# Layer 1's attention logits formed on TensorE in a four-layer graph network on one Trainium2 core

## The chip, the cores and the metric

The kernel runs on one core of one Trainium2 chip, as one launch. Its time is the device time of that core in microseconds; the figure of a kernel is the median over several executions. The profile is of one execution, with its own time. Its abbreviations: PE is TensorE's matmuls and PEld its weight loads, DVE is VectorE, ACT is ScalarE, POOL is GpSimd, SP is SyncE, which issues most DMAs.

## The reference

Sixteen graphs of 1024 nodes with 64 features each go through four layers, each of the form x + layer(relu(layernorm(x))). The change is in layer 1, a graph attention layer:

```
def layer1(inp, adj, W, a):                       # inp: relu(layernorm(x)), [16, 1024, 64]
    h = einsum('bnf,fo->bno', inp, W)
    lh = leaky_relu(h, negative_slope=0.2)
    f_src = lh @ a[:64, 0]
    f_dst = lh @ a[64:, 0]
    e = f_src[:, :, None] + f_dst[:, None, :]
    dj = 0.8 * adj + 0.2 * e
    attention = softmax(where(dj > 0, dj, -1e12), axis=1)
    return relu(einsum('bij,bjo->bio', attention, h))
```

So every node has two logits, f_src and f_dst, and a column j of the attention matrix is a masked softmax over the source nodes i. Layer 0 is a plain product with adj, layer 2 a hyperbolic attention layer, and layer 3 takes weighted quantiles of every node's neighbours (which the kernel does by sorting) followed by a small MLP.

## The kernel before

**Tiling.** A graph's 1024 nodes lie as 8 tiles (NT) of 128 partitions (P), features along the free dimension (C = 64). The adjacency matrix comes from memory transposed, one tile of 128 x 1024 at a time, through `Feed`, which keeps three tiles in flight. Partition p of tile J is node j = 128 J + p, and its row holds all sources i.

**Streams.** The program is written as generators, called streams, that run at build time: `heads` (layers 0, 1 and 2 of every graph, as `fast0`, `fast1` and `fast2`), `places` (drops neighbours and ranks the rest, mostly f16 matmuls into PSUM tiles pv and pd), `weigh`, `fetches` (GpSimd's indirect DMAs that gather neighbours' rows, la and hg), `hubs` and `lows` (sorting networks of `max` and `min` on VectorE, tiles ha, hb, la and lb) and `finish` (the MLP). After each piece a stream yields the tiles that it needs next. The loop at lines 2355 to 2365 always steps the ready stream with the smallest due time. A `Plan` (lines 80 to 173) books every instruction at a cost from formulas and says when a tile will be ready. A head counts as HEADS_US = 127 us of VectorE, a graph's hubs as 82, its lows as 93. Hubs and lows start 1.3 graphs behind. On each engine the instructions then stand in exactly the order in which they were laid out (`Queue`), and the real waits are semaphores.

**Gates.** Layer 2 of a graph waits until its ranking is done (`T.ranked > b`, line 1655), which `places` does beside layer 1; fetches of a graph wait until its head is done (`T.headed > b`); lows and hubs wait for what was fetched.

**Layer 1, `fast1` (line 1315).** After the layer norm, h is transposed to hT (64 x 1024), one half at a time through one PSUM tile pt. Eight matmuls with the weights wgs give ph = h W with nodes on partitions, which ScalarE copies to hp. VectorE then forms lh = max(0.2 hp, hp) and two dot products over the features (a product with a row of `a` broadcast to all partitions, asr or adr, and a reduction): fs and fd, one column per tile. fs is scaled by 0.25, and two more tiny operations give thr = -0.25 fd and fd2 = 0.2 fd. In the trace fd2 is written fd, since trailing digits are left out of names. TensorE transposes fs, broadcast along the free dimension, which puts the row of all fs on all 128 partitions; ScalarE copies it to fsr, which has hT's memory.

Then comes a loop over the tiles J of adj, software-pipelined: `attend` (one pass of VectorE, d = adj + fsr with the row's maximum mx; CUSTOM_DVE_ANT_0 in the trace, with an accumulator read behind it), `bound` (nm = min(-0.8 mx, fd2)), `exponential` (ScalarE, exp(0.8 d + nm)), `chosen` (VectorE's second pass, keeping ex where d > thr and summing it to sm), `share` (1 / sm to rs), ScalarE's hs = hp rs, and two matmuls with hs as weights into pa. In a step the first pass of column J comes before the second pass of column J - 1, and `bound` of J comes behind it:

Of the kernel before, what the change touches and what calls it, by code (L numbers as in the profile page):

```python
# [17 lines left out]
F32 = mybir.dt.float32  # L18
# [275 lines left out]
def tile_gnn_stack(  # L294
# [109 lines left out]
    def bcast_row(src, name):  # L404
        t = cp.tile([P, src.shape[-1]], F32, name=name)
        nc.sync.dma_start(t, src.partition_broadcast(P))
        return t
# [3 lines left out]
    wgs = cp.tile([C, C], F32, name="wgs")  # L411
# [7 lines left out]
    nc.sync.dma_start(w2s, w2)  # L419
    b1s = cp.tile([H, 1], F32, name="b1s")  # L420
    nc.sync.dma_start(b1s, b1)
    b0r = bcast_row(b0, "b0r")
    b2r = bcast_row(b2, "b2r")
    asr = bcast_row(ag[0], "asr")
    adr = bcast_row(ag[1], "adr")
# [5 lines left out]
    def row3(r):  # L431
        return r[:, None, :].to_broadcast([P, NT, C])
# [53 lines left out]
    def transpose_steps(dst, src, ps, tag, bufs):  # L486

        R, pts = src.shape[2], []
        for hf in range(2):
            pt = ps.tile([P, HN], F32, tag=tag, name="pt")  # L490
            for k in range(4):
                nc.tensor.transpose(pt[:R, k * P:(k + 1) * P], src[:, 4 * hf + k, :], ident)
            pts.append(pt)
            if hf or bufs == 1:
                for k in range(len(pts)):
                    yield [pts[k]]
                    h0 = hf if bufs == 1 else k
                    nc.scalar.copy(dst[:, h0 * HN:(h0 + 1) * HN], pts[k][:R, :])
                pts = []
# [773 lines left out]
    def halves(po, lhs, rhs, J):  # L1273

        for hf in range(2):
            nc.tensor.matmul(po[64 * hf:64 * hf + 64, :], lhs, rhs[:, hf * HN:(hf + 1) * HN],
                             start=(J == 0), stop=(J == NT - 1))
# [36 lines left out]

    def fast1(feed, xt, xn):
        with tc.tile_pool(name="f1", bufs=1) as sp, tc.tile_pool(name="f1w", bufs=2) as wp, \
                tc.tile_pool(name="f1p", bufs=1, space=PSUM) as ps:
            h = sp.tile([P, NT, C], F32, name="h")
            yield from norm_steps(h, xt, sp, "ln_xc")
            hT = sp.tile([C, N], F32, tag="hT", name="hT")  # L1320
            yield from transpose_steps(hT, h, ps, "pt", 1)
            yield [hT]
            ph = ps.tile([P, NT, C], F32, name="ph")
            for t in range(NT):
                nc.tensor.matmul(ph[:, t, :], hT[:, t * P:(t + 1) * P], wgs, start=True, stop=True)
            yield [ph]
            hp = sp.tile([P, NT, C], F32, name="hp")
            nc.scalar.copy(hp, ph)
            yield [hp]
            lh = sp.tile([P, NT, C], F32, name="lh")  # L1330
            nc.vector.scalar_tensor_tensor(lh, hp, 0.2, hp, ALU.mult, ALU.max)
            fs = sp.tile([P, NT], F32, name="fs")
            dot(fs, lh, row3(asr), sp, "dot")
            fd = sp.tile([P, NT], F32, name="fd")
            dot(fd, lh, row3(adr), sp, "dot")

            nc.vector.tensor_scalar_mul(fs, fs, 0.25)
            thr = sp.tile([P, NT], F32, name="thr")
            nc.vector.tensor_scalar_mul(thr, fd, -0.25)
            fd2 = sp.tile([P, NT], F32, name="fd2")  # L1340
            nc.vector.tensor_scalar_mul(fd2, fd, 1.0 - 0.8)
            fsr = sp.tile([P, N], F32, tag="hT", name="fsr")
            for hf in range(2):
                yield [fs, fsr] if hf else [fs]
                pt = ps.tile([P, HN], F32, tag="pt", name="pt")
                for k in range(4):
                    t = 4 * hf + k
                    nc.tensor.transpose(pt[:, k * P:(k + 1) * P], fs[:, t:t + 1].to_broadcast([P, P]), ident)
                yield [pt]
                nc.scalar.copy(fsr[:, hf * HN:(hf + 1) * HN], pt)  # L1350
            yield

            pa = ps.tile([P, HN], F32, name="pa")
            mx = sp.tile([P, NT], F32, name="mx")
            nm = sp.tile([P, NT], F32, name="nm")
            sm = sp.tile([P, NT], F32, name="sm")
            def attend(J, a):
                one_ = slice(J, J + 1)
                d = wp.tile([P, N], F32, name="d")
                nc.vector.tensor_tensor_reduce(d, a, fsr, 1.0, -3.0e38, ALU.add, ALU.max, mx[:, one_])  # L1360
                return d

            def bound(J):
                one_ = slice(J, J + 1)
                nc.vector.tensor_scalar(nm[:, one_], mx[:, one_], -0.8, fd2[:, one_], ALU.mult, ALU.min)

            def exponential(J, d):
                one_ = slice(J, J + 1)
                ex = wp.tile([P, N], F32, name="ex")
                nc.scalar.activation(ex, d, AF.Exp, bias=nm[:, one_], scale=0.8)  # L1370
                return ex

            def chosen(J, d, ex):
                one_ = slice(J, J + 1)
                nc.vector.scalar_tensor_tensor(ex, d, thr[:, one_], ex, ALU.is_gt, ALU.mult, accum_out=sm[:, one_])

            def share(J):
                one_ = slice(J, J + 1)
                rs = wp.tile([P, 1], F32, name="rs")
                nc.vector.tensor_scalar_max(rs, sm[:, one_], 0.5)  # L1380
                nc.vector.reciprocal(rs, rs)
                return rs

            d = ex = None
            for J in range(NT + 1):
                e = d
                if J < NT:
                    a = feed.next()
                    yield [a, fsr] + [ex] * (J > 0)
                    d = attend(J, a)  # L1390
                elif J:
                    yield [ex]
                if J:
                    chosen(J - 1, e, ex)
                x = ex
                if J < NT:
                    bound(J)
                if J:
                    rs = share(J - 1)
                    yield [rs]  # L1400
                    hs = wp.tile([P, C], F32, name="hs")
                    nc.scalar.activation(hs, hp[:, J - 1, :], AF.Copy, scale=rs)
                if J < NT:
                    ex = exponential(J, d)
                if J:
                    yield [hs]
                    halves(pa, hs, x, J - 1)
            yield []
            z = sp.tile([P, NT], F32, name="z")
            nc.vector.tensor_scalar(z, sm, 0.5, 1.0 / N, ALU.is_lt, ALU.mult)  # L1410
            yield [z]
            pu = ps.tile([P, 1], F32, name="pu")
            for hf in range(2):
                for J in range(NT):
                    nc.tensor.matmul(pu[64 * hf:64 * hf + 64, :], hp[:, J, :], z[:, J:J + 1], start=(J == 0), stop=(J == NT - 1))
            yield [pu]
            us = sp.tile([P, 1], F32, name="us")
            nc.scalar.copy(us, pu)
            r = sp.tile([P, HN], F32, name="r")
            nc.scalar.activation(r, pa, AF.Relu, bias=us)  # L1420
            yield [r]
            po = ps.tile([P, 4, 2, C], F32, tag="ph", name="po")
            for k in range(4):
                nc.tensor.transpose(po[:, k].rearrange("p h c -> p (h c)"), r[:, k * P:(k + 1) * P], ident)
            yield
            v = "p (h k) c -> p k h c"
            nc.vector.tensor_tensor(xn.rearrange(v, h=2), po, xt.rearrange(v, h=2), ALU.add)
# [989 lines left out]
```

## Time and profile before

| | us |
|---|---|
| median of 3 runs | 5802.13 |
| lowest, highest | 5785.95, 5806.57 |
| span of the profiled execution | 5801.1 |
| granted TensorE clock, mean | 0.624 |

The groups of instructions that the change touches, with their counts over the 16 graphs (busy us in all, mean ns of one):

| group | count | busy us | mean ns |
|---|---|---|---|
| VectorE lh<-hp | 16 | 11.1 | 696 |
| VectorE dot_pr<-lh,asr and dot_pr<-lh,adr | 16 each | 11.1 each | 693, 691 |
| VectorE fs<-dot_pr and fd<-dot_pr | 16 each | 11.0 each | 686 |
| VectorE nm<-mx,fd | 128 | 26.5 | 207 |
| VectorE d<-adj,fsr (first pass) | 128 | 155.6 | 1216 |
| VectorE ex<-d,thr,ex (second pass) | 128 | 164.7 | 1287 |
| TensorE pt<-ident,fs | 128 | 32.3 | 402 |
| TensorE ph<-wgs,hT | 256 | 58.8 | 421 |

How to read it: a group is named out<-in by tiles, and a TensorE f32 matmul of the program shows as two instructions. Busy time is the sum of durations; neighbouring instructions of an engine may overlap a little, so that the distance from one start to the next can be shorter than the duration. A view in order of time lists each instruction's start and duration in us, and in brackets the idle time of its engine before it. A view of waits lists who waited for which tile of which engine: us in total, times, longest.

### The profile page before, as it was taken

Reading aid. Unit: us, or ns where it says so; the run is one execution under the profiler, and the core shown is the slowest. Engines: PE = TensorE matmul, PEld = TensorE weight load, DVE = VectorE, ACT = ScalarE, POOL = GpSimd, SP = SyncE. Lnnn points to the kernel's source line nnn. Section 1 sums busy time; section 2 is a strip of 40 time slices with the busy share of each in tenths; the row PEclk is TensorE's granted clock in tenths of the full one; section 3 lists DMA queues with packets and bytes.
Section 4 is the critical chain, followed back from the end, with each engine's and each line's share of the span. In section 5 each row is a group of like instructions: output and inputs, shape, how many; then the busy total and the mean of one; then the engine's idle time right before and its main releaser. Section 6 shows DMA issues by size and latency. Waiting matters only on the chain. (4 is left out here: it accounts for less than half of the span.)

```text
span 5801.1 us, 60310 instructions
## 1 busy us (share of the span) xinstructions
PE 3195.6 (55%) x13232; PEld 1786.9 (31%) x13233; DVE 5107.1 (88%) x13854; ACT 3240.9 (56%) x9555; POOL 3698.0 (64%) x2903
## 2 busy tenths in 40 slices
PE   6566564646746464764646656474665646566110
PEld 2334242323423233342323324233342323324000
DVE  3579989999899999899899998999989899898857
ACT  4555565656556565565556556565655556565312
POOL 0174675758657574875758667576876758677676
PEclk7766656666665666666566665666666566666555
DMA  2232322223232222322323242322323222242120
GB/s 70 63 89 62 103 59 78 70 76 89 68 88 71 75 70 63 102 68 76 77 74 72 66 103 58 78 71 71 92 68 84 67 76 69 65 104 66 30 46 15
DMA packets 460779, 419.38 MB, mean 72 GB/s; under 512 B 218067, under 2 KB 351667, under 8 KB 460404
## 3 DMA queue, kind: packets, MB, share of 16 engines
q1 hardware_dynamic: 353908, 295.94, 17.8%
q0 software_dynamic: 106496, 119.49, 10.5%
q8 instruction: 107, 1.75, 0.1%
q14 instruction: 268, 2.20, 0.1%
HBM read 363.99 MB, written 50.54 MB: 71 GB/s over the span
## 5 line engine op out<-in xcount | busy, mean ns | idle before, releaser
L187 POOL DMA_INDIRECT la<-s_hd,ix x1856 | 2405.5, 1296 | 1351.4 <-DVE ix L187 698.6
L187 POOL DMA_INDIRECT hg<-s_hd,ix x768 | 990.7, 1290 | 234.0 <-issue 211.5
L187 DVE TENSOR_TENSOR lb<-la 128x128 f32<-128x128 f32 (+14 forms) x1760 | 677.0, 438 | 83.5 <-DMA la<-s_hd,ix 44.8
L187 DVE TENSOR_TENSOR la<-lb 128x256 f32<-128x256 f32 (+11 forms) x1856 | 695.9, 431 | 51.8 <-ACT lb L187 48.1
L187 DVE TENSOR_TENSOR hb<-ha 128x128 f32<-128x128 f32 (+36 forms) x1632 | 637.4, 447 | 53.0 <-ACT ha L187 29.1
L187 DVE TENSOR_TENSOR ha<-hb 128x64 f32<-128x64 f32 (+36 forms) x1568 | 606.5, 441 | 5.0 <-ACT hb L187 4.0
L187 PE MATMUL pw<-ident,u_z 128*128 128x128 f32 x1024 | 237.4, 376 | 441.1 <-DVE u_z L187 430.0
L187 POOL DMA_INDIRECT s_vp<-vr,s_place x128 | 154.3, 1206 | 432.6 <-DVE c_sb L187 144.3
L187 PE MATMUL pm<-w,hn 128*65 128x128 f32 x2048 | 405.9, 380 | 6.1 <-DVE w L187 5.8
L187 PE MATMUL pd<-tab_r,tab_dist 67*128 67x512 f32 x512 | 381.6, 838 | 23.6 <-DVE u_g L187 12.4
L187 PEld LDWEIGHTS pm<-w,hn 128*65 128x65 f32 x2048 | 388.3, 210 | 9.4 <-DVE w L187 9.4
L187 PEld LDWEIGHTS pw<-ident,u_z 128*128 128x128 f32 x1024 | 170.5, 193 | 648.6 <-issue 573.9
L187 PE MATMUL pl<-tab_ll,tab_rl 66*128 66x512 f32 x512 | 367.4, 809 | 0.0
L187 ACT COPY hb<-ha 128x32 f32<-128x32 f32 (+24 forms) x1280 | 274.4, 284 | 144.5 <-DVE ha L187 140.6
L187 PE MATMUL pf<-vcol,one 128*1 128x3 f32 x32 | 3.1, 166 | 633.5 <-DVE vcol L187 633.5
L187 ACT ACTIVATE u_g<-pd,gxc 128x512 f32<-128x512 f32 x256 | 174.5, 682 | 315.4 <-PE pd L187 294.3
L187 ACT COPY ha<-hb 128x4 f32<-128x4 f32 (+22 forms) x1264 | 253.3, 268 | 172.6 <-DVE hb L187 169.5
L187 PE MATMUL pv<-wtile,krow 8*128 8x512 f16 x512 | 290.3, 567 | 103.4 <-ACT d L187 55.8
L187 PE MATMUL pa<-adj,h 128*64 128x512 f32 x512 | 196.8, 895 | 246.6 <-DMA adj<-in_adjt 124.3
L187 ACT COPY lb<-la 128x64 f32<-128x64 f32 (+6 forms) x784 | 195.4, 296 | 205.0 <-DVE la L187 102.8
L187 PE MATMUL pv<-wt,ng 128*128 128x128 f16 x2048 | 297.2, 295 | 0.0
L187 DVE FIND_INDEX8 ix<-seek,row 128x8 uint32<-128x1056 f16 x224 | 279.7, 1250 | 0.0
(342 smaller groups left out, 8282.0 us busy)
## 6 DMA issues: line engine op xcount, KB each, us to landing
adj<-in_adjt SPq DMA_DIRECT2D x384, 512.0 KB
la<-s_hd,ix POOLq DMA_INDIRECT x1856
row<-s_vp SPq DMA_DIRECT2D x112, 256.0 KB
hg<-s_hd,ix POOLq DMA_INDIRECT x768
wb<-wd SPq DMA_DIRECT2D x32, 342.0 KB
row<-s_vp SPq DMA_DIRECT2D x192, 28.0 KB
row<-s_vp SPq DMA_DIRECT2D x192, 24.0 KB
xa<-in_x SPq DMA_DIRECT2D x16, 256.0 KB
```

Source lines behind the costliest of these rows:

```text
L187: r = f(*a, **k)
```

## The change

The logits come from TensorE. Since leaky_relu(v) = 0.2 v + 0.8 relu(v), a logit is 0.2 (W a) . h + 0.8 a . relu(h W). One constant tile `aside` (128 x 2) holds both sets of coefficients, one above the other, already multiplied by 0.25 for the source logit and by 0.2 for the destination logit. It is made once, before the streams start, from two small loads of `a`, a transpose of W and one matmul.

In `fast1` the tile `cat` (128 x 1024) takes hT in its upper half of partitions and relu(h W), transposed, in its lower half: two matmuls with wgs as weights give (h W) transposed for 512 nodes each, and ScalarE's relu copies them. Two matmuls with a column of `aside`, broadcast as 128 equal columns, give the source logits already on all partitions, and ScalarE copies them to fsr. Eight matmuls with tiles of `cat` as weights and the other column of `aside` give the destination logits, one column each; a copy makes them fd. lh, both dot products, the three scalings and the eight transposes of fs go.

In the loop the first pass forms d = -0.8 (adj + fsr) and takes the minimum, beginning with the node's fd. Its accumulator is then nm itself, and `bound` goes. The exponential is exp(nm - d), and the second pass keeps ex where d < fd. The pool of PSUM tiles has two slots for pt, which pa uses too, where there were one for pt and one for pa.

```diff
+    aside = cp.tile([P, 2], F32, name="aside")
+    agt = ag.rearrange("k c -> c k")
+    nc.sync.dma_start(aside[C:2 * C], agt)
+    with tc.tile_pool(name="wa", bufs=1) as kp, tc.tile_pool(name="wap", bufs=1, space=PSUM) as kps:
+        a0 = kp.tile([C, 2], F32, name="a0")
+        nc.sync.dma_start(a0, agt)
+        pw = kps.tile([C, C], F32, name="pw")
+        nc.tensor.transpose(pw, wgs, ident[0:C, 0:C])
+        wgt = kp.tile([C, C], F32, name="wgt")
+        nc.scalar.copy(wgt, pw)
+        pwa = kps.tile([C, 2], F32, name="pwa")
+        nc.tensor.matmul(pwa, wgt, a0, start=True, stop=True)
+        for k, f in enumerate((0.25, 1.0 - 0.8)):
+            nc.vector.tensor_scalar_mul(aside[0:C, k:k + 1], pwa[:, k:k + 1], 0.2 * f)
+            nc.vector.tensor_scalar_mul(aside[C:2 * C, k:k + 1], aside[C:2 * C, k:k + 1], (1.0 - 0.2) * f)
...
-            hT = sp.tile([C, N], F32, tag="hT", name="hT")
-            yield from transpose_steps(hT, h, ps, "pt", 1)
-            yield [hT]
-            ph = ps.tile([P, NT, C], F32, name="ph")
+            cat = sp.tile([P, N], F32, name="cat")
+            yield from transpose_steps(cat[0:C], h, ps, "pt", 2)
+            yield [cat]
+            ph = ps.tile([P, NT, C], F32, name="ph", bufs=1)
             for t in range(NT):
-                nc.tensor.matmul(ph[:, t, :], hT[:, t * P:(t + 1) * P], wgs, start=True, stop=True)
-            yield [ph]
+                nc.tensor.matmul(ph[:, t, :], cat[0:C, t * P:(t + 1) * P], wgs, start=True, stop=True)
+            pts = []
+            for hf in range(2):
+                pt = ps.tile([P, HN], F32, tag="pt", name="pt", bufs=2)
+                nc.tensor.matmul(pt[C:2 * C, :], wgs, cat[0:C, hf * HN:(hf + 1) * HN], start=True, stop=True)
+                pts.append(pt)
+            for hf in range(2):
+                yield [pts[hf]]
+                nc.scalar.activation(cat[C:2 * C, hf * HN:(hf + 1) * HN], pts[hf][C:2 * C, :], AF.Relu)
+            yield [cat]
+            fsr = sp.tile([P, N], F32, name="fsr")
+            pts = []
+            for hf in range(2):
+                pt = ps.tile([P, HN], F32, tag="pt", name="pt", bufs=2)
+                nc.tensor.matmul(pt, aside[:, 0:1].to_broadcast([P, P]), cat[:, hf * HN:(hf + 1) * HN], start=True, stop=True)
+                pts.append(pt)
+            pf = ps.tile([P, NT], F32, tag="pu", name="pf", bufs=1)
+            for t in range(NT):
+                nc.tensor.matmul(pf[:, t:t + 1], cat[:, t * P:(t + 1) * P], aside[:, 1:2], start=True, stop=True)
+            for hf in range(2):
+                yield [pts[hf]]
+                nc.scalar.copy(fsr[:, hf * HN:(hf + 1) * HN], pts[hf])
+            yield [pf]
+            fd = sp.tile([P, NT], F32, name="fd")
+            nc.scalar.copy(fd, pf)
             hp = sp.tile([P, NT, C], F32, name="hp")
             nc.scalar.copy(hp, ph)
-            yield [hp]
-            lh = sp.tile([P, NT, C], F32, name="lh")
-            nc.vector.scalar_tensor_tensor(lh, hp, 0.2, hp, ALU.mult, ALU.max)
-            fs = sp.tile([P, NT], F32, name="fs")
-            dot(fs, lh, row3(asr), sp, "dot")
-            fd = sp.tile([P, NT], F32, name="fd")
-            dot(fd, lh, row3(adr), sp, "dot")
-
-            nc.vector.tensor_scalar_mul(fs, fs, 0.25)
-            thr = sp.tile([P, NT], F32, name="thr")
-            nc.vector.tensor_scalar_mul(thr, fd, -0.25)
-            fd2 = sp.tile([P, NT], F32, name="fd2")
-            nc.vector.tensor_scalar_mul(fd2, fd, 1.0 - 0.8)
...
-                for k in range(4):
-                    t = 4 * hf + k
-                    nc.tensor.transpose(pt[:, k * P:(k + 1) * P], fs[:, t:t + 1].to_broadcast([P, P]), ident)
-                yield [pt]
-                nc.scalar.copy(fsr[:, hf * HN:(hf + 1) * HN], pt)
-            yield
+            yield [fsr, fd]
...
-                nc.vector.tensor_tensor_reduce(d, a, fsr, 1.0, -3.0e38, ALU.add, ALU.max, mx[:, one_])
+                nc.vector.tensor_tensor_reduce(d, a, fsr, -0.8, fd[:, one_], ALU.add, ALU.min, nm[:, one_])
                 return d
-
-            def bound(J):
-                one_ = slice(J, J + 1)
-                nc.vector.tensor_scalar(nm[:, one_], mx[:, one_], -0.8, fd2[:, one_], ALU.mult, ALU.min)
...
-                nc.scalar.activation(ex, d, AF.Exp, bias=nm[:, one_], scale=0.8)
+                nc.scalar.activation(ex, d, AF.Exp, bias=nm[:, one_], scale=-1.0)
...
-                nc.vector.scalar_tensor_tensor(ex, d, thr[:, one_], ex, ALU.is_gt, ALU.mult, accum_out=sm[:, one_])
+                nc.vector.scalar_tensor_tensor(ex, d, fd[:, one_], ex, ALU.is_lt, ALU.mult, accum_out=sm[:, one_])
...
-                if J < NT:
-                    bound(J)
```

More of the change, by code (lines that the diff above doesn't have):

```diff
@@ L1316, in fast1 @@
         with tc.tile_pool(name="f1", bufs=1) as sp, tc.tile_pool(name="f1w", bufs=2) as wp, \
-                tc.tile_pool(name="f1p", bufs=1, space=PSUM) as ps:
+                tc.tile_pool(name="f1p", bufs=2, space=PSUM) as ps:
             h = sp.tile([P, NT, C], F32, name="h")
             yield from norm_steps(h, xt, sp, "ln_xc")
-            hT = sp.tile([C, N], F32, tag="hT", name="hT")
-            yield from transpose_steps(hT, h, ps, "pt", 1)
-            yield [hT]
-            ph = ps.tile([P, NT, C], F32, name="ph")
+            cat = sp.tile([P, N], F32, name="cat")
@@ L1340, in fast1 @@
-            fd2 = sp.tile([P, NT], F32, name="fd2")
-            nc.vector.tensor_scalar_mul(fd2, fd, 1.0 - 0.8)
[L1342 to L1345, printed above, removed]
-                for k in range(4):
-                    t = 4 * hf + k
-                    nc.tensor.transpose(pt[:, k * P:(k + 1) * P], fs[:, t:t + 1].to_broadcast([P, P]), ident)
-                yield [pt]
-                nc.scalar.copy(fsr[:, hf * HN:(hf + 1) * HN], pt)
@@ L1351, in fast1 @@
-            yield
-            pa = ps.tile([P, HN], F32, name="pa")
-            mx = sp.tile([P, NT], F32, name="mx")
+            yield [fsr, fd]
+            pa = ps.tile([P, HN], F32, tag="pt", name="pa", bufs=2)
             nm = sp.tile([P, NT], F32, name="nm")
@@ L1411, in fast1 @@
             yield [z]
-            pu = ps.tile([P, 1], F32, name="pu")
+            pu = ps.tile([P, 1], F32, name="pu", bufs=1)
             for hf in range(2):
@@ L1421, in fast1 @@
             yield [r]
-            po = ps.tile([P, 4, 2, C], F32, tag="ph", name="po")
+            po = ps.tile([P, 4, 2, C], F32, tag="ph", name="po", bufs=1)
             for k in range(4):
```

## The prediction

> **What bounds the kernel now.** I read the page from the top: busy shares, then the slices, then stretches of the span, then the order of time inside one graph.
>
> ```profile
> PE 3195.6 (55%) x13232; PEld 1786.9 (31%) x13233; DVE 5107.1 (88%) x13854; ACT 3240.9 (56%) x9555; POOL 3698.0 (64%) x2903
> DVE  3579989999899999899899998999989899898857
> 2000.00:2500.00 500.00, 304.14 (x1332) 164.74 (x1332) 462.94 (x1289) 302.75 (x905) 347.42 (x277) 0.62 0.30 75
> 5400.00:5801.00 401.00, 29.41 (x84) 16.39 (x84) 293.65 (x843) 110.05 (x489) 275.58 (x180) 0.50 0.16 32
> POOL la L187 <- DVE ix L187: 698.6, 26, 65.5
> 2360.00:2390.00 30.00, 25.51 (x122) 0.52 0.32 66
> ```
>
> Lines 1 and 2: VectorE is the fullest engine, and its empty slices are the first three and the last few. Line 3, a stretch of the middle (columns: PE, PEld, DVE, ACT, POOL busy, granted clock, DMA share, GB/s): 463 of 500 us on VectorE. The view of waits between 1000 and 5000 us names some 239 us of 4000 in which VectorE waited for another engine or a DMA; the rest of its gaps are fractions of a microsecond between dependent instructions. So the middle runs at VectorE's pace. The op that begins layer 1's logits (lh) starts at 1016.0 us in graph 3 and 5156.3 us in graph 15: 345 us a graph. What leaves VectorE there leaves the span. Line 4, the tail after the last head: VectorE is idle 107 us of 401, and GpSimd's row fetches pace it. Line 5: GpSimd waits 699 us in all for indices, 26 times, mostly because the next graph's head has not ended. Line 6, TensorE alone in 30 us around graph 7's logits: 25.5 busy at a granted clock of 0.52. In that stretch TensorE is nearly full. The chain of waits covers only the last 24 us (the MLP of graph 15), which the change doesn't touch.
>
> **What leaves VectorE.** Graph 7, in order of time (start, duration):
>
> ```profile
> 2374.36 0.69 DVE L187 SCALAR_TENSOR_TENSOR lh<-hp 128x512 f32<-128x512 f32 x1
> 2375.09 0.69 DVE L187 TENSOR_TENSOR dot_pr<-lh,asr 128x512 f32<-128x512 f32 x1
> 2375.81 0.69 DVE L187 TENSOR_REDUCE fs<-dot_pr 128x8 f32<-128x512 f32 x1
> 2376.53 0.69 DVE L187 TENSOR_TENSOR dot_pr<-lh,adr 128x512 f32<-128x512 f32 x1
> 2377.26 0.69 DVE L187 TENSOR_REDUCE fd<-dot_pr 128x8 f32<-128x512 f32 x1
> 2377.86 0.17 DVE L187 TENSOR_SCALAR fs<-fs 128x8 f32<-128x8 f32 x1
> 2377.98 0.17 DVE L187 TENSOR_SCALAR thr<-fd 128x8 f32<-128x8 f32 x1
> 2378.06 0.16 DVE L187 TENSOR_SCALAR fd<-fd 128x8 f32<-128x8 f32 x1
> 2378.14 0.08 DVE L187 MATCH_VALUE_LOAD ix<-seek,row 128x8 f16 x1
> ...
> 2395.05 1.27 DVE L187 SCALAR_TENSOR_TENSOR ex<-d,thr,ex 128x1024 f32<-128x1024 f32 x1
> 2396.25 0.08 DVE L187 DVE_READ_ACCUMULATOR ex<-d,thr,ex 128x1 f32 x1
> 2396.25 0.20 DVE L187 TENSOR_SCALAR nm<-mx,fd 128x1 f32<-128x1 f32 x1
> 2396.38 0.14 DVE L187 TENSOR_SCALAR rs<-sm 128x1 f32<-128x1 f32 x1
> ```
>
> All eight ops from lh to the last fd go. I count them from start to start, because neighbours overlap: 2378.14 - 2374.36 = **3.8 us a graph**. Nothing of another stream stands between them, so nothing fills the hole but the next work.
>
> [...] In columns 1 to 7 nm starts with the accumulator read and rs follows 0.13 us later; rs reads that accumulator, and where a result of the accumulator read is wanted at once (graph 7's column 0: read at 2387.32, nm at 2387.44) the reader starts 0.12 us after it. So nm sits in a gap that rs would leave anyway: about 0.01 us. Only column 0, with no such rs, frees 0.2 us. I take **0.2 us a graph**.
>
> **What VectorE gets.** Each of the 128 first passes (mean 1216 ns, CUSTOM_DVE_ANT_0) now starts its accumulation at a column of fd instead of a literal, with a minimum instead of a maximum. The trace has neither form. Lower bound 0: as many elements and passes. Upper bound by rows: rs<-sm, 128x1 with literals, 144 ns; nm, 128x1 with a column among its operands, 207 ns; so +63 ns. The second pass, which has a column operand, takes 1.20 us to its accumulator read, the first 1.15: +50 ns. I take 50 ns, 8 x 0.05 = **0.4 us a graph**; the exponential's and the second pass's other signs cost nothing.
>
> Sum on VectorE: 3.8 + 0.2 - 0.4 = 3.6 us a graph, x 16 = **58 us**. By busy durations it would be 3.95 + 1.66 - 0.4 = 5.2, x 16 = 83 us: the upper end. The lower end, with the pointer at 63 ns and the bounds at nothing, is 53 us.
>
> **What TensorE gets.** New per graph: two calls of hT by W (512 columns), two of the broadcast logit column (512 columns), eight that give the destination logit (one column each). Gone: eight transposes of fs. A 512-column f32 call of layer 2 (pd, pl) goes from start to start in 0.86 us at best and 1.58 us for the first of a row of them; at this stretch's clock of 0.52 I take 1.6, four calls 6.4 us. The eight one-column calls have a close row:
>
> ```profile
> 155.39 3.57 PE L187 MATMUL pq<-attc,tab_r 64*128 64x2 f32 x16
> ```
>
> Eight calls, each with its own 128-wide weights, two instructions per call: 3.57 us. [...] The row decides: 3.5. The transposes took 4 in 1.06 us, so 2.0 come back. Net 6.4 + 3.5 - 2.0 = **+7.9 us a graph** (4.9 at the best spacing), 126 us in all on an engine 55% busy.
>
> What waits there: TensorE's broadcast call waits for ScalarE's relu of both halves; behind it on TensorE stand the ranking matmuls (pv) of the same graph's places, behind these ScalarE's d and VectorE's rem. ScalarE's copy of fd waits for all eight one-column calls, and the first pass waits for that copy. In graph 7 the first column started 16.1 us after the first ph matmul (2370.04 to 2386.17). The new chain: ph 3.6, hT by W 3.2, last relu 0.58 (row hT<-pt), broadcasts 3.2, one-column calls 3.5, copies of fd and hp 0.7: 14.8 us, plus ranking matmuls laid between (up to 5 us). VectorE has other streams' work meanwhile, as it has now; if that cover were gone, the delay would cost up to 4 us a graph. In graphs 0 and 1, where VectorE is half idle, the two chains are equal within that, so the 3.6 us may be lost there: 7 us at most.
>
> **What else.** ScalarE: two relus of 0.58 and one small copy (0.16, row us<-pu), 1.3 us a graph on an engine 56% busy: hidden. Set-up, once: two small loads on SP (0.4 to 0.8 us of issue, before an xa load that SP issues only at 20.02, when VectorE's set-up ends), a transpose, a copy and a matmul beside POOL's set-up, four tiny VectorE ops of 0.19: +0.8 us. The logit tiles take the two slots that pt and pa had, so nothing new waits for PSUM.
>
> **The order.** The streams are laid out by booked costs, so every later instruction may move. By the code's own formulas the head is booked 3.9 us less and, if the column counts as a third operand, 1.4 more for the first passes: -2.5 of HEADS_US = 127, which stays. Heads then gain 2% on hubs and lows, up to 0.3 graph by the end. That moves 0.3 x (82 + 93) = 52 us of sorting behind the last head. If the 107 idle us of the tail take it, the gain is up to 52 us; if GpSimd's fetches, 0.3 of some 270 us a graph, are late with it, the loss is 81 - 52 = 29 us. Gates hold streams together, so I take 0.
>
> Sum against the profiled execution: 5801.1 - 58 + 0.8 = 5744; half of the first two graphs' 7 us given back, 5748. The median before, 5802.13, is 1 us above that span, so the same sum serves both.
>
> **The rivals.** (1) **Given back by the new order.** For it: GpSimd's and the tail's 29 us above, static waits of ScalarE copies (la, lb, ha: some 67 us in the middle) that may fall elsewhere. Against: VectorE's waits are 6% only. 5748 + 29 = 5777, up to 5830 if waits grow by another 53 us. (2) **TensorE's ranking stretch sets the pace.** Place: line 6 above, 85% full; places must end before layer 2 of the same graph, and GpSimd already waits for heads. Price: heads later by 7.9 us a graph, less the 3.6 that VectorE frees: 16 x 4.3 = +69, so 5870. It decides from the point where VectorE finds no sorting to do, that is where its share in the middle falls below some 91% while GpSimd's waits for indices grow. Against: that share is 92 to 93% now and sorting has buffers of up to three fetched blocks. (3) **All busy time counts**, and the tail takes the heads' lead: 5801 - 83 = 5718, down to 5690. (4) The minimum form of the pass costs a second sweep or the like, 128 x 1.2 = +154: 5900; nothing in the trace speaks for it, and it is counted within the slower chance.
>
> **How the numbers follow.** About 0.5% (29 us) can be told from no change. Forecast 5748, own range 5725 to 5772: 0.50. Rival 3: 0.12. Rival 1: 0.20, mostly within 29 us of before. Rivals 2 and 4: 0.18. Faster 0.62, same 0.20, slower 0.18. The range leaves out most of rivals 2 and 4 and the end of rival 3: 5700 to 5840.
>
> **What would show it.** VectorE busy down by about 83 us by the page though the span falls less; the custom pass at 1.21 to 1.28 us; rs still 0.12 us behind its accumulator read; one-column matmuls at 3.5 us for eight; ph-to-first-pass within 15 to 20 us; a period of some 341 us. Wrong if the pass exceeds 1.35 us, if GpSimd's waits for indices grow by over 60 us, or if the middle's VectorE share drops below 91%.

## The result and the profile after

The changed kernel takes 5834.34 us (median of 6 runs, 5819.18 to 5847.72) against 5802.58 us for the kernel before in the same job (6 runs, 5785.77 to 5808.61): ratio 1.0067, 95% interval 1.0051 to 1.0084. It is slower by 0.7%, where faster by 0.9% was forecast. The profiled execution has a span of 5845.9 us at a mean granted clock of 0.626, so 44.8 us more than before; it is the slowest of its six runs, and the medians lie 31.8 us apart.

The page of the kernel after, busy time of the engines and VectorE's slices:

```profile
PE 3287.0 (56%) x13491; PEld 1839.6 (31%) x13492; DVE 5047.6 (86%) x13602; ACT 3265.9 (56%) x9604; POOL 3624.8 (62%) x2903
DVE  3579989899898989989898898989989898998957
```

VectorE's busy time fell by 5107.1 - 5047.6 = 59.5 us. Its idle time (span less busy) rose from 694.0 to 798.3, by 104 us. The work did leave. More than that came back as gaps, and the slices show where: in the middle every second or third digit is now an 8.

The stretches (columns: length, PE, PEld, DVE, ACT, POOL busy, granted clock, DMA share, GB/s). Line 1 is the middle of the kernel before. The others are of the kernel after: the middle, one stretch of it, the tail, 30 us around graph 7's logits, and the densest stretch of graph 7's ranking:

```profile
1000.00:5000.00 4000.00, 2354.91 (x9676) 1313.75 (x9675) 3672.86 (x9917) 2346.25 (x6843) 2680.78 (x2101) 0.62 0.30 76
1000.00:5000.00 4000.00, 2381.22 (x9815) 1334.30 (x9814) 3600.15 (x9698) 2345.70 (x6868) 2599.05 (x2095) 0.63 0.29 75
2000.00:2500.00 500.00, 308.83 (x1297) 163.50 (x1297) 450.55 (x1229) 283.93 (x857) 342.37 (x271) 0.63 0.31 83
5400.00:5845.90 445.90, 68.37 (x239) 43.80 (x237) 332.26 (x923) 130.78 (x535) 296.40 (x207) 0.53 0.16 34
2410.00:2440.00 30.00, 24.59 (x100) 13.06 (x100) 25.93 (x67) 21.69 (x47) 24.52 (x19) 0.57 0.28 67
2476.00:2513.00 37.00, 35.98 (x160) 18.93 (x160) 33.46 (x79) 18.01 (x41) 28.77 (x28) 0.50 0.21 47
```

VectorE's share of the middle is 90.0%; before it was 3672.9 of 4000 us, 91.8%. The tail starts later (the last head ends 61 us later) but is itself 16 us shorter. In line 5, around graph 7's logits as in the prediction, TensorE is no fuller than before (24.59 us against 25.51). Line 6 is a stretch that the prediction did not consider: 35.98 of 37 us busy at a granted clock of 0.50.

VectorE's waits between 1000 and 5000 us, with GpSimd's wait for indices over the whole run from the same view (us in all, times, longest):

```profile
DVE la L187 <- ACT lb L187: 74.7, 54, 2.4
DVE lb L187 <- DMA la<-s_hd,ix: 40.2, 13, 4.4
DVE v_a L187 <- ACT v_l L187: 38.5, 12, 4.7
...
DVE rt_r L187 <- ACT rt_s L187: 31.2, 24, 2.4
...
POOL la L187 <- DVE ix L187: 810.2, 18, 59.1
```

Before, these four of VectorE were 22, 0, 6 and 5 us, and GpSimd's wait was 698.6. All of VectorE's named waits in the middle add to 309 us, against 239 before. No single wait holds the loss. VectorE waits more for ScalarE's copies and for fetched rows, and GpSimd waits 112 us more for the next head: the heads come later.

So I measured the heads stage by stage: distances between the first instructions of each stage, mean over graphs 3 to 14, in us. Layer 1 runs from its layer norm to its last operation. The ranking goes on beside it: its first part runs from its first to its second group of pc matmuls, its second part from there to the last copy to krow. The MLP counts as inside when its last matmuls (py) begin there.

| | before | after |
|---|---|---|
| period | 345.3 | 348.3 |
| layer 1 | 109.3 | 113.3 |
| layer 2 waits, after layer 1's last operation | 2.6 | 9.9 |
| layer 2 | 187.5 | 180.5 |
| from there to the next layer 1 | 45.9 | 44.7 |
| ranking, first part | 65.6 | 74.7 |
| ranking, second part | 40.7 | 50.5 |
| graphs (of 16) with the MLP inside the second part | 1 | 14 |

The four rows below the period add up to it. It grows by 3.0 us, 48 us over 16 graphs, near the 44.8 us between the profiled executions. Layer 1 is 4.0 us longer, layer 2's wait for the ranking 7.3 us longer, and layer 2 itself 7.0 us shorter. The last row points to a cause of the wait. The MLP is that of an earlier, finished graph (`finish`), and the change doesn't touch it. Here is TensorE in order of time in graph 7 of the kernel after (start, duration):

```profile
2476.99 1.92 PE L187 MATMUL pt<-ident,ga 128*64 128x128 f32 x8 [2.00 <-DVE ga L187]
2478.83 2.07 PE L187 MATMUL ph<-ot,w1s 64*128 64x512 f32 x2
2480.84 0.60 PE L187 MATMUL pv<-wtile,krow 8*128 8x512 f16 x1
...
2482.98 2.07 PE L187 MATMUL ph<-ot,w1s 64*128 64x512 f32 x2
...
2489.03 3.68 PE L187 MATMUL py<-w2s,hid 128*128 128x64 f32 x16
2492.64 0.60 PE L187 MATMUL pv<-wtile,krow 8*128 8x512 f16 x1
...
2516.67 1.94 PE L187 MATMUL pk<-ident,n_key 128*128 128x128 f32 x8 [3.71 <-DVE n_key L187]
```

The rows with ga, w1s and w2s are the MLP: 1.92 + 2.07 + 2.07 + 3.68 = 9.74 us, between ranking matmuls (pv) that stand back to back from 2478.8 to 2513. The ranking's second part is 50.5 - 40.7 = 9.8 us longer. Its beginning does have gaps: over the whole second part, in the mean of graphs 3 to 14, TensorE is busy 83% at a granted clock of 0.61 (82% at 0.63 before). In the kernel before, the last matmuls of graph 7's ranking and its MLP's py were these:

```profile
2459.95 1.94 PE L187 MATMUL pk<-ident,n_key 128*128 128x128 f32 x8 [1.30 <-DVE n_key L187]
L187 PE MATMUL py<-w2s,hid x16: 315/421/421, 2490.2 to 2493.3; 128*128 128x64 f32 x16
```

The ranking's matmuls ended at 2461.9, and py began 28 us later, beside layer 2, where no one waited for it.

### The profile page after: what moved, and what is told of

It reads as the page before. It is cut to its first block, busy times and chain, and to the rows that moved or that the text cites. A ratio compares the mean times of both kernels' runs of the same rounds, so it can differ in the third digit from the quotient of the medians.

```text
span 5845.9 us, 60160 instructions
## 1 busy us (share of the span) xinstructions
PE 3287.0 (56%) x13491; PEld 1839.6 (31%) x13492; DVE 5047.6 (86%) x13602; ACT 3265.9 (56%) x9604; POOL 3624.8 (62%) x2903
## 5 line engine op out<-in xcount | busy, mean ns | idle before, releaser
L187 POOL DMA_INDIRECT la<-s_hd,ix x1856 | 2288.8, 1233 | 1466.2 <-DVE ix L187 810.2
L187 POOL DMA_INDIRECT hg<-s_hd,ix x768 | 1013.2, 1319 | 234.0 <-issue 206.0
L187 POOL DMA_INDIRECT s_vp<-vr,s_place x128 | 173.5, 1355 | 438.5 <-DVE c_sb L187 147.6
L187 PE MATMUL pv<-wtile,krow 8*128 8x512 f16 x512 | 284.1, 555 | 95.3 <-ACT d L187 80.0
```

Source lines behind the costliest of these rows:

```text
L187: r = f(*a, **k)
```

## The experiments

Ratios are to the kernel before of the same job, with their 95% intervals. The kernel before had medians of 5761 to 5809 us in the six jobs, so runs of different jobs (e1 to e4, e5 to e8, e9 to e12, e13 to e16, e17 and e18) are compared by their ratios. "Gate" is used below for one edit in two streams: `places` counts the rankings begun, and `finish`, ahead of the MLP, waits until none is under way. It adds no instruction, but whatever is laid out behind it may change its place too:

```diff
         ng, ps = T.flagged.pop(b)
+        T.begun += 1
...
             nc.vector.tensor_tensor(ga, ga, hl, ALU.add)
+            yield lambda: self.ranked == self.begun
             yield [ga]
```

**The halves of the change.** e1 has the logits from TensorE (the change's diff down to `yield [fsr, fd]`) and the loop of before, with one tiny operation for thr; e2 the logits of before and the new loop, of which this is the first pass:

```diff
-                nc.vector.tensor_tensor_reduce(d, a, fsr, 1.0, -3.0e38, ALU.add, ALU.max, mx[:, one_])
+                nc.vector.tensor_tensor_reduce(d, a, fsr, -0.8, fd2[:, one_], ALU.add, ALU.min, nm[:, one_])
```

> Logits by TensorE as in the changed kernel, but the loop of the kernel before (maximum from a literal, bound as an operation of its own, second pass against thr). Theory A (the added TensorE work in front of and between the ranking matmuls makes the ranking end later, and layer 2 waits for the ranking): as slow as the changed kernel or a little more, 5825 to 5850 us, and from the start of layer 1 to the end of the ranking about 125 us a graph as in the changed kernel (106 before). Theory B (any change of the booked costs moves the order away from one that happened to fit): slower than before by an amount that does not follow the TensorE work, with this run and the one that changes only the loop both slower by 20 us or more. Theory D (the pass with a column as its start and the missing bound are what costs): near 5745 to 5760 us.

> Logits by VectorE as before, but the changed loop (the first pass begins its minimum at the node's column, no bound, second pass against the same column). Theory A: the time of before within 10 us, 5793 to 5812, since 128 passes cost 59 ns more each (0.47 us a graph) and the bound and thr give 0.2 to 0.4 us back; the ranking ends about 106 us after the start of layer 1. Theory B: slower than before by 20 us or more. Theory D: 5830 us or more.

e1: 1.0192 [1.0170, 1.0213]; VectorE busy 5056.6, idle 819.1. e2: 1.0098 [1.0077, 1.0120]; busy 5109.8, idle 727.0. One half is slower than the whole and the other no faster, so the parts don't add up. e2's busy time is 2.7 us above that of before, where its 128 first passes cost 7.6 us more (1275 ns for 1216): without the bounds and thr, whose durations add to over 26 us, VectorE is busy only some 5 us less. Both halves lose by idle time, and the MLP lies in the ranking's second part in 14 graphs (e1) and 10 (e2). In e2 the second part takes 50.2 us, but layer 2 waits only 2.1 us, no longer than before, so the MLP adds no wait of layer 2 there.

**The MLP moved out of the ranking.** e3 is the kernel after with the gate, e5 the kernel before with it.

> The changed kernel, with one gate more: the MLP of a finished graph is laid out only when no ranking is under way, so that its 9.7 us of TensorE work cannot stand between ranking matmuls. Theory A in its full form (TensorE's queue in the ranking stretch decides, whoever fills it): the ranking ends some 10 us earlier, about 115 us after the start of layer 1, and the time falls to 5740 to 5790 us. If only the logits' own matmuls matter: 5825 to 5845. Theory B: any value, with no tie to the ranking's end.

> The kernel before with the gate that lays out a finished graph's MLP only when no ranking is under way. In the trace of before, 15 of the 16 MLPs lie outside a ranking anyway, so theory C (what the slower kernels lose is in part MLPs that fall into the ranking's second part) expects the time of before within 15 us, with the second part of the ranking at 38 to 41 us as before. Theory B (luck of the order) allows anything.

e3: 1.0014 [1.0003, 1.0025]; e5: 1.0016 [1.0001, 1.0031]. The gate does nothing for the kernel before and takes back 0.5% in the changed one: the second part of the ranking falls from 50.5 to 38.1 us, layer 2's wait from 9.9 to 1.8 and the period from 348.3 to 344.7.

**TensorE work alone.** e4 puts four matmuls, whose results nobody uses, behind ph in the kernel before; e7 adds the gate to it; e6 is e2 with the gate.

```diff
+            pw = ps.tile([P, HN], F32, tag="pt", name="pw")
+            for k in range(4):
+                nc.tensor.matmul(pw[0:C, :], wgs, hT[:, (k % 2) * HN:(k % 2 + 1) * HN], start=True, stop=True)
             yield [ph]
```

> The kernel before with four more 512-column f32 matmuls of W and hT right behind the matmuls of h W, whose result nobody reads: some 7 us of TensorE work a graph at the place where the change puts its own, and nothing else. Theory A: the ranking ends 7 to 10 us later (113 to 117 us after the start of layer 1), and the time rises by 30 to 110 us, 5830 to 5910. If TensorE has room there: 5795 to 5810.

> The kernel before with the four idle matmuls behind those of h W, plus the gate. Theory C with A: the first part of the ranking stays about 9 us longer (74 instead of 65.6 us), the second goes back to 40, and what is left over the kernel before with the gate is the price of 7 us of TensorE work a graph alone: 0 to 60 us, against 93 us without the gate. If the gate gives nothing here: 5860 or more.

> Only the loop changed (logits by VectorE), plus the same gate. Without the gate this loop took 1.0 per cent more than before, with 9 of 16 MLPs inside a ranking and a second part of 50 us on average. Theory C: the second part goes back to some 40 us and the time to within 15 us of the kernel before with the gate, 40 us or more below the run without it. Theory B or a slow first pass: it stays near 1.01 of before.

e4: 1.0175 [1.0144, 1.0207], with the MLP in the second part in 14 graphs. About 7 us a graph of useless TensorE work in layer 1 (an estimate: two such calls took 3.67 us in graph 7 of the kernel after), and nothing else of the change, brings a loss, larger than that of the change, and the MLP's move. e7: 1.0097 [1.0061, 1.0133], so the gate gives back 0.8%, and 45 us (5840.12 - 5794.75) remain over e5. e6: 1.0088 [1.0056, 1.0120] where e2 had 1.0098; there the gate shortened the second part from 50.2 to 35.7 us and gave nothing; layer 2's wait, short before, stayed so (2.3). e2's loss isn't explained by the MLP.

**Is VectorE's time worth its length?** e8 is e5 with six passes more of VectorE a graph, in `lows`.

```diff
+            for _ in range(6):
+                nc.vector.tensor_tensor(aggl[:, 0:7], aggl[:, 0:7], aggl[:, 0:7], ALU.max)
             self.lowed += 1
```

> The kernel before with the gate, and in every graph six more VectorE passes over 448 columns at the end of the low sorts (maximum of a tile with itself, 3.7 us a graph by durations): the same amount of VectorE work that the change takes out, put in at a place that no head waits for. The prediction's theory (the middle runs at VectorE's throughput): +50 to +60 us over the kernel before with the gate. Theory E (the chain of the heads sets the pace, and work in other streams fills gaps): +0 to +20 us.

1.0134 [1.0100, 1.0167]: 67 us more than e5 for 60.6 us more of busy time. In this one order, work added to VectorE counts about one to one, as the forecast's basis has it. It is no proof: an order alone moved the time by 64 us (e12, below).

**The booking.** e9 is e3 with the plan's costs of the new matmuls set to what the trace shows (order only). e10 is e3 with the relu half of the logits left out: two of the four wide matmuls and both relus go, and the other new matmuls use 64 rows of `cat`. So its logits are only their linear part. Their edits, in this order:

```diff
             if reads[0].dtype in (F16, BF):
                 c = max(0.07, n * 0.0008)
+            elif n == 1:
+                c = 0.23
+            elif out.shape[0] == 64 and n == HN and reads[0].shape[0] == 64:
+                c = 1.83
```

```diff
-                nc.tensor.matmul(pt[C:2 * C, :], wgs, cat[0:C, hf * HN:(hf + 1) * HN], start=True, stop=True)
...
-                nc.scalar.activation(cat[C:2 * C, hf * HN:(hf + 1) * HN], pts[hf][C:2 * C, :], AF.Relu)
...
-                nc.tensor.matmul(pf[:, t:t + 1], cat[:, t * P:(t + 1) * P], aside[:, 1:2], start=True, stop=True)
+                nc.tensor.matmul(pf[:, t:t + 1], cat[0:C, t * P:(t + 1) * P], aside[0:C, 1:2], start=True, stop=True)
```

> The changed kernel with the gate on the MLP, and with TensorE's booked costs set to what the traces show: 1.83 us for each of the two 512-column products of W and hT (booked 0.85), 0.23 us for a one-column matmul (booked 0.42 for the eight of the destination logit and next to nothing for the sixteen of pu). Not one instruction differs, only the order on each engine. Theory F (the layout believes the relu's input ready 2 us too early, ScalarE then stands still at the relu with the sorts' copies behind it, and VectorE waits for those): VectorE's stalls between the start of layer 1 and its first pass fall from 50 us in 4000 to some 25, and the time from the 1.001 of the gated kernel to 0.993 to 0.997. If the stalls are not due to the booking: 1.000 to 1.004.

> The changed kernel with the gate, the relu half of the logits left out: logits from the 64 upper rows only, so the two products of W and hT and ScalarE's two relus go, 3.7 us of TensorE a graph and a wait of ScalarE. Everything else stays. The output is not the reference's, since the logits are only their linear part. Theory A/F (that TensorE work and the wait on it cost): VectorE's stalls in the stretch before the first pass at 20 to 35 us in 4000, the first part of the ranking at 66 to 70 us, the time at 0.990 to 0.996 of before. Theory B: anywhere within one per cent.

e9: 1.0012 [0.9997, 1.0026], no different from e3; the theory behind it had 0.993 to 0.997, and fell. e10: 1.0067 [1.0042, 1.0091], slower than e3 with less to do. Its layer 1 is 9.0 us a graph shorter (105.6 against e3's 114.6), but the ranking is not (112.9 us from its first pc group to krow, against 112.3). So 5.9 us come back as layer 2's wait, with no MLP in the ranking, and layer 2 is 4.7 us longer, for which no cause was found. A single pair of kernels is then too little to judge by.

**Other orders.** So two constants that only set the order (how late a stream may be stepped, and how far GpSimd is kept ahead) were varied, with the same instructions: first in the kernel before.

```diff
-LATE_US = 5.0
+LATE_US = 4.0
```

```diff
-AHEAD_US = 16.0
+AHEAD_US = 20.0
```

> The kernel before with one scheduling constant changed (LATE_US 4 in place of 5): exactly the same instructions in another order. It measures how much the order alone is worth. Theory B: slower than before by 10 to 60 us, with more VectorE stalls and the same busy time. If the order before is nothing special: within 10 us either way.

> The kernel before with another scheduling constant changed (AHEAD_US 20 in place of 16): the same instructions in another order, a second sample beside the one with LATE_US 4. Theory B: slower by 10 to 60 us. Otherwise within 10 us either way.

Then at the same settings in the kernel after, and with AHEAD_US 12 in both:

```diff
-AHEAD_US = 16.0
+AHEAD_US = 12.0
```

> The kernel after with LATE_US 4 for 5: the same instructions, another order. The kernel before with that setting came to 1.0004. Theory work (TensorE's logits and the MLP behind them hold VectorE's streams up at any order): slower than before at the same setting by 0.3 to 1.0%, so 1.003 to 1.010. Theory order (the change is worth its 1% of VectorE time, and the order laid out for it was an unlucky one): the orders of the changed kernel scatter around 0.99, and this one is as likely below 1 as above it: 0.985 to 1.000.

> The kernel after with AHEAD_US 20 for 16: the same instructions, another order. The kernel before with that setting came to 1.0108. Theory work: 1.013 to 1.020, as the change adds its own loss to that of the setting. Theory order: no relation to the setting's effect on the kernel before; 0.985 to 1.010.

> The kernel before with AHEAD_US 12 for 16: the same instructions, another order; it is what the next run is to be read against. Theory work says nothing of it. Theory order: before's order as it stands is among the good ones (VectorE idle 693 us, 666 to 819 seen), so this one is the same or slower: 1.000 to 1.012.

> The kernel after with AHEAD_US 12 for 16: the same instructions, another order. Theory work: slower than the kernel before with AHEAD_US 12, of the same shared run, by 0.3 to 1.0%. Theory order: not slower than that, 0.985 to 1.000 of the kernel before.

And the changed kernel with the gate, at the two settings where its loss was largest beside a good time before:

> The kernel after with AHEAD_US 12 and with the MLP of a finished graph held until no ranking is under way, as in e3. Without that gate it came to 1.0222, and the kernel before at this setting to 1.0054; in its trace the MLP's matmuls are to be found in the ranking's second part in most graphs. Theory MLP (the largest part of the loss is the MLP that lies in the ranking's second part and keeps layer 2 waiting): 1.003 to 1.010. Theory logits (the largest part is TensorE's logit work itself, ahead of the ranking's first part): 1.016 to 1.022.

> The kernel after with LATE_US 4 and with the same gate. Without the gate it came to 1.0242, and the kernel before at this setting to 1.0004; 14 of its 16 MLPs lie in the ranking's second part. Theory MLP: 0.998 to 1.006. Theory logits: 1.016 to 1.024.

In each cell the ratio to the kernel before as it stands, its interval, and in how many graphs the MLP lies in the ranking's second part:

| order | before | after | after with the gate |
|---|---|---|---|
| as laid out (LATE 5, AHEAD 16) | 1; 1 graph | 1.0067 [1.0051, 1.0084]; 14 | e3: 1.0014 [1.0003, 1.0025]; 0 |
| LATE 4 | e11: 1.0004 [0.9992, 1.0015]; 1 | e13: 1.0242 [1.0214, 1.0270]; 14 | e18: 0.9982 [0.9964, 1.0001]; 0 |
| AHEAD 12 | e15: 1.0054 [1.0039, 1.0068]; 5 | e16: 1.0222 [1.0196, 1.0249]; 14 | e17: 0.9943 [0.9926, 0.9960]; 0 |
| AHEAD 20 | e12: 1.0108 [1.0085, 1.0131]; 1 | e14: 1.0214 [1.0181, 1.0247]; 14 | not run |

The loss isn't bad luck of one order: at four settings of four the changed kernel is slower than the kernel before, by 0.7 to 2.4%, with the MLP in the ranking in 14 graphs each time, and the order that the change came with was the best of its four. The losses of e13 and e16 are larger than either theory had given. At three settings of three the gate takes all or most of the loss away, 0.5, 2.6 and 2.8%, though all of TensorE's new work is still there. The theory that this work costs the time by itself gave 1.016 and more for e17 and e18, and fell.

By what path the gate helps is less clear. As laid out, it shortens layer 2's wait by 8.1 us and the period by 3.6. At LATE 4 and AHEAD 12 the periods fall by 11.8 and 10.0 us, the waits only by 5.4 and 4.6. And in 13 of e16's 14 graphs only py lies in the second part, the rest of the MLP just ahead of it. Graph 7 of e16, its py and a later ranking matmul:

```profile
L187 PE MATMUL py<-w2s,hid x16: 275/275/323, 2484.2 to 2485.9; 128*128 128x64 f32 x16
2495.98 0.58 PE L187 MATMUL pv<-wtile,krow 8*128 8x512 f16 x1 [6.17 <-ACT vr L187]
```

The 2.0 us of py don't make that second part 11 us longer than e17's. TensorE stands idle for 6.17 us in it: ScalarE's copy to vr comes, in its fixed order, behind an hs that waits 4.38 us for VectorE. So the gate is shown to take the loss away. That it does so by the MLP's own time on TensorE fits the order as laid out, and at AHEAD 12 it doesn't. A gate on some other stream, which would tell the MLP's place from the new order that comes with any gate, was not run.

e17 beats both kernels. Its page, and below it its MLP in graph 7 and GpSimd's wait for indices:

```profile
PE 3343.0 (58%) x13491; PEld 1860.8 (32%) x13492; DVE 5049.2 (87%) x13602; ACT 3254.1 (56%) x9604; POOL 3610.3 (62%) x2903
```

```profile
L187 PE MATMUL py<-w2s,hid x16: 421/421/473, 2488.8 to 2492.1; 128*128 128x64 f32 x16
```

```profile
POOL la L187 <- DVE ix L187: 632.9, 19, 52.8
```

VectorE has the same work as in the kernel after, the span is 5776.8 us, and GpSimd waits 177 us less for heads. TensorE in order of time shows a ranking without the MLP in it, from the second pc group to pk:

```profile
2439.40 3.62 PE L187 MATMUL pc<-ng,sel 128*8 128x512 f16 x16
...
2471.85 0.60 PE L187 MATMUL pv<-wt,ng 128*128 128x128 f16 x4
2472.25 1.06 PE L187 MATMUL po<-ident,r 128*128 128x128 f32 x4
...
2474.23 1.94 PE L187 MATMUL pk<-ident,n_key 128*128 128x128 f32 x8
```

Its matmuls end at 2476.2, and py begins 12.6 us later. The same stages for the settings with AHEAD 12 (means over graphs 3 to 14, us):

| | e15, before | e16, after | e17, after with the gate |
|---|---|---|---|
| period | 345.4 | 353.0 | 343.0 |
| layer 1 | 116.7 | 117.2 | 115.5 |
| layer 2 waits | 3.0 | 6.4 | 1.8 |
| layer 2 | 179.3 | 184.0 | 179.2 |
| from there to the next layer 1 | 46.4 | 45.4 | 46.5 |
| ranking, first part | 71.1 | 77.1 | 81.4 |
| ranking, second part | 42.7 | 47.2 | 36.0 |

Of the three, e17 has the longest first part and the shortest period: the longer first part did no harm there.

The gain of 0.57% rests on little: e17 is the best of three gated orders, and the kernel before with both the gate and AHEAD 12 was not run. Over the three gated orders the changed kernel stands at 0.9980 on average, and the kernel before without the gate at 1.0019 at the same three settings.

## Why the prediction was wrong

**What leaves VectorE: right.** The sum by starts was 58 us, and the page's busy time fell by 59.5. The 83 us under what would show it was a wrong yardstick: it has the bounds at 1.66 us a graph, their durations in the profile of before (26.5 us / 16), and the page counts overlapping stretches once (from 2439.53 to 2441.20 us of the rows below it has 1.60 us busy, where the durations, with the reciprocal behind rs, add to some 1.8), so it fell by the starts too. The loop of graph 7 of the kernel after, VectorE in order of time:

```profile
2438.33 1.27 DVE L187 CUSTOM_DVE_ANT_0 d<-adj,fsr,fd 128x1024 f32<-128x1024 f32 x1
2439.53 0.08 DVE L187 DVE_READ_ACCUMULATOR2_ANT nm<- 128x1 f32 x1
2439.53 1.27 DVE L187 SCALAR_TENSOR_TENSOR ex<-d,fd,ex 128x1024 f32<-128x1024 f32 x1
2440.74 0.08 DVE L187 DVE_READ_ACCUMULATOR ex<-d,fd,ex 128x1 f32 x1
2440.85 0.15 DVE L187 TENSOR_SCALAR rs<-sm 128x1 f32<-128x1 f32 x1
```

With nm gone, rs still starts 0.11 us behind the accumulator read that it needs. The bound sat in that gap, as the row said, and e2 agrees: its 128 bounds and 16 thr freed some 5 us of the 26.5 us that the bounds' durations add to. The pass has a mean of 1275 ns against 1216: 59 for the 50 assumed, under the bound of 63.

**What TensorE gets: near, with two errors of opposite sign.** Graph 7 of the kernel after, TensorE in order of time:

```profile
2414.13 3.67 PE L187 MATMUL ph<-wgs,cat 64*128 64x64 f32 x16
2417.74 3.67 PE L187 MATMUL pt<-cat,wgs 64*64 64x512 f32 x4
...
2425.49 3.10 PE L187 MATMUL pt<-cat,aside 128*128 128x512 f32 x4
2428.43 1.84 PE L187 MATMUL pf<-aside,cat 128*128 128x1 f32 x16
```

3.67 + 3.10 + 1.84 - 2.0 for the transposes is +6.6 us, where 7.9 was worked out. The four wide calls took 6.8 (6.4 assumed), the eight one-column calls 1.84 (3.5 assumed). The row pq that I took was the wrong neighbour. The trace of before has a nearer one in the same graph: pu<-z,hp, 128x1 with 32 instructions in 3.17 us, so 1.6 for 16.

**Hidden by other streams' work: held in the main.** From ph to the first pass it was 20.4 us in graph 7 (15 to 20 forecast), 20.8 against 18.7 in the mean, and layer 1 as a whole is 4.0 us longer. But VectorE stood idle right ahead of its 128 first passes for only 6.0 us in all (3.2 before), and at the other two settings layer 1 is about as long with the change and the gate as before (e18 114.5 and e11 113.8, e17 115.5 and e15 116.7).

**The order: this step failed.** "Gates hold streams together, so I take 0." The prediction asked what the new order does among heads, hubs and lows, as a lead of the heads, and there little could change: the costs that the plan books on VectorE for a head sum to 95.3 us before and 92.8 after, both far under HEADS_US = 127, so heads come first either way. What moved was `finish`, a stream that the prediction named only for its tail. Extra TensorE work in layer 1 is enough to bring its matmuls into the ranking's second part in 14 graphs of 16 (shown by e4), and layer 2 waits at a gate for that ranking. Measured by taking the MLP out, the term is some +31 us at the order as laid out (1.0067 against 1.0014), and +151 and +162 us at the other two settings (e13 against e18, e16 against e17), not 0; these are differences of ratios, times 5802. At the order as laid out, 86 us lie between the forecast of 5748 and the median of 5834. The 31 us are accounted for so, and the other 55 are not.

**The rivals.** Rival 2, TensorE's ranking stretch sets the pace, named the place, and both of its signs came: VectorE's middle share is under 91% and GpSimd's waits for indices grew by more than 60 us. Its 5870 lies 24 us above the profiled span. Its mechanism was half right. The ranking does hold layer 2 up, but not by the logits' work alone, which e17 and e18 keep without a loss; at the order as laid out, the MLP's 9.7 us lie in it. Rival 1 had the kind of cause, a static order that gives the gain back, with no place for it. Its far end, 5830, is near the measured 5834. Rival 3 fell with the sign of the result, and rival 4 is out: the pass takes 1275 ns, 59 more than before, where the rival had 1.2 us more.

**What stays open.** How the added work leads to the MLP's place follows from the layout at build time, and was not traced through it. What else the gate's new order does at LATE 4 and AHEAD 12 is not separated from the MLP's place. With the MLP out of the way the changed kernel gains 1.1% over the kernel before at one setting, 0.2% at another and loses 0.1% at the third, where the VectorE sum says 1%. e7's 45 us suggest that TensorE's time has a price of its own, but orders differ by up to 1.1% in the kernel before (e12) and 1.7% in the changed one (e13) with no instruction changed, so that part isn't shown. The loss of the loop alone (e2, e6) has no cause found.

## What to carry to other kernels

In a program whose engines run a fixed order, work put on an engine "with room" can cost by what it pushes, which may be another stream altogether (here 1.8% for e4's four calls on an engine 55% busy). Before forecasting, list every stream that uses the engine, find the stretch whose end someone waits for at a gate, and ask what could slide into it. Judge such a change at several orders, and on both kernels at each, because one order can be worth as much as the change (here 1.1% in e12, where the change lost 0.7%). Where a piece of work has no deadline, as this MLP, a gate that keeps it out of that stretch is worth a try: here it cost the kernel before about 0.2% and took all or most of the changed kernel's loss away at three orders, though only one of them brought the forecast gain.

## What the hardware showed

- The 128x1024 first pass became 59 ns longer (1216 to 1275 ns, 128 passes) when its accumulation started from a column of memory instead of a literal, with a minimum instead of a maximum and the factor -0.8 instead of 1.0. No run separates the three. Two tiny operations, with and without a column operand, lie 63 ns apart (207 and 144 ns).
- The eight f32 calls of one column with new 128-wide weights each (pf, graph 7 of the kernel after) take 1.84 us in a row, 115 ns for each of the 16 instructions, while the profile gives each a duration of 167 to 251 ns, mostly 251. Here the sum of single durations is about twice the length of the row.
- In the densest 37 us of graph 7's ranking TensorE is 97% busy at a granted clock of 0.50, where the mean of the execution is 0.626: the stretch with the least slack ran at less than the mean clock.
